# Attention stretches of two head pairs with sixteen products between, in a masked-attention and graph-convolution kernel

## Chip, cores and metric

The kernel runs on one core of a Trainium2 chip. The metric is the device time of one launch in microseconds (us); lower is better.

## What is computed

For each of 32 batches, `x` has 512 rows of 512 features; one 512 x 512 adjacency `adj` serves all. The reference, cut to what matters:

```python
# layer 0: attention with 8 heads of 64, masked by adj
q, k, v = x @ Wq + bq, x @ Wk + bk, x @ Wv + bv
scores = einsum('bihd,bjhd->bhij', q, k) / 8 + where(adj == 0, -1e9, 0)
out = einsum('bhij,bjhd->bihd', softmax(scores), v)
x = layernorm(x + out)
# layer 1: graph convolution with the normalized adjacency
norm_adj = adj * rsqrt(deg)[:, None] * rsqrt(deg)[None, :]
x = layernorm(x + einsum('nm,bmo->bno', norm_adj, x @ weight) + bias)
```

## The kernel before, in words

Everything is in the function `unshifted`. The wrapper `InOrder` pins the instructions of TensorE (PE, matmuls), VectorE (DVE), ScalarE (ACT) and GpSimd (POOL) to the order in which the program issues them; since every one of them passes through its line 44, the profile shows L44 for all, and groups are told apart by their tiles. SyncE (SP) issues nearly all DMAs.

**Blocks.** The work of attention is cut into `S` = 128 blocks: `blocks[k]` is batch `b` = k // 4 and one pair of heads (`ORDER`, line 821); `at` = k % 4. `G` is 4. A block has these parts:

- `scores((b, g, jj))`, lines 395 to 409, is called for jj 0 and 1. Each call makes two score tiles of 128 x 1024 (two heads by 512 columns). PE multiplies with 64 rows of the array for each head (`sc<-kq`), DVE takes the tile out of PSUM with the mask (`e<-sc,maskT`), ACT makes the exponential in place (`e<-e`). PSUM has three "wide" buffers (`WIDE`, bufs=3) for these tiles; SBUF has six `e` buffers.
- `values((b, g, jj))`, lines 430 to 468, multiplies V with the exponentials, with 64 columns of the array for each head (`av<-e,v`). After jj = 1, DVE transposes the result into the single buffer `yb`, and four DMAs carry it to `YT`.
- `accumulate`, lines 411 to 428, sums the exponentials on POOL (`acc`). The sums of the first call are made at once; those of the second are put on the list `pending`, and a piece `put_off` of the side work makes one of them (`more`, line 814). What is left is made at the start of the next block.
- `fold`, lines 470 to 480, transposes and reduces `acc` on DVE (`acc<-acc`, `folded<-acc`), one block later.

**Products.** Between the blocks PE does the projections of the next batch and the graph convolution of the last one. A piece of side work that counts more than 1 is a product: one PSUM bank filled by eight matmul instructions of 128 rows and 128 columns and evicted by DVE or ACT. `bank` (line 98) gives products PSUM buffers in a fixed turn: the three wide ones, then a narrow one. A batch has 32 products: seven for V (`values_of`), seven for each half of K and Q (`keys_and_queries`), four with the adjacency (`first` of `convolve`, eight matmuls of 512 columns each), seven with the second weight (`second`).

**The order.** The loop over k (line 847) is written out by hand. In the turn of block k the program issues `scores` 0 of k, `fold` of k - 1, `scores` 1 of k, `values` 0 and 1 of k - 1, `accumulate` 0 of k, and then `shares.pop(0)`, one share of side work. At `at` = 1 a batch's side work is planned: `main` lists the products, `beside` (a dictionary by the index of the product) says which small steps follow which product, and `cut(side, counts)` (line 799) cuts the list into shares of so many products. Before, each of four blocks gets a share of eight. There too, SP is given the loads of `x` and of the residual.

**The steps in `beside` that matter here** belong to the layer norm of batch b - 1 (`finish`, line 520): `inverse` and `scale` (DVE) divide by the sums, `add` (POOL) adds the residual, `measure` (DVE, `st`, `mv`) takes the statistics, `root` (DVE `ve`, `nmu`, then POOL `rstd`, `add`) makes scale and shift, `norm` (ACT) writes `yT` and the rounded part `hi`, `low` (DVE) writes the rest `lo`. `rest` holds `measure`, `root` and `store` of the convolution before. A `keys_and_queries` product 0 is evicted by ACT into `e1` (`e<-mm,bias`), and product 1 of the same seven adds its bank to that `e1` on DVE (`kq<-e,mm`).

The functions that the change touches, with the line numbers of the profile:

Of the kernel before, what the change touches and what calls it, by code (L numbers as in the profile page):

```python
# [49 lines left out]
def unshifted(  # L50
# [32 lines left out]
    G = H // 2  # L83
# [83 lines left out]
    def load_residual(b):  # L167

        if b < B - 2:
            t = acts.tile([P, NT, D], F32, name="xr", tag="zT", bufs=1)  # L170
            R[b] = [t[:, i, :] for i in range(NT)]
        elif b == B - 2:
            t = [acts.tile([P, 2, D], F32, name="xr2", tag=tag, bufs=n) for tag, n in (("x", 1), ("kq", 5))]
            R[b] = [t[i // 2][:, i % 2, :] for i in range(NT)]
        else:
            R[b] = [wk[:, i].rearrange("p u o -> p (u o)") for i in range(NT)]
        for i in range(NT):
            nc.sync.dma_start(R[b][i], x[b, ts(i, P), :])
# [210 lines left out]
    def turns(b):  # L389

        return [(0, turn, (b, 0))], [(0, turn, (b, 1))] + [(0, combine, (b, k)) for k in range(4)]
# [3 lines left out]
    def scores(s):  # L395

        b, g, jj = s
        E[s] = [work.tile([P, 2, N], F32, name="e", bufs=6) for _ in range(2)]
        for l in range(2):
            j = 2 * jj + l  # L400
            e = E[s][l]
            p = psum.tile([P, 2, N], F32, name="sc", **WIDE)
            for k in range(2):
                r = slice(k * HD, (k + 1) * HD)
                tensor.matmul(p[:, k, :], KQ[b, g][r, 0, ts(j, P)], KQ[b, g][r, 1, :], start=True, stop=True)
            vector.scalar_tensor_tensor(
                e, p, CUT, maskT[:, j, None, :].to_broadcast([P, 2, N]), op0=ALU.min, op1=ALU.subtract
            )
            scalar.activation(e, e, AF.Exp)
# [389 lines left out]
    def cut(pieces, counts):  # L799

        lists = [[]]
        left = list(counts)
        for piece in pieces:
            if piece[0] > 1:
                if not left[0]:
                    left.pop(0)
                    lists.append([])
                left[0] -= 1
            lists[-1].append(piece)
        return lists  # L810
# [3 lines left out]
    def more():  # L814

        if pending:
            accumulate(*pending.pop(0))

    put_off = [(0, more, ())]

    ORDER = (0, 2, 1, 3)
    blocks = [(b, g) for b in range(B) for g in ORDER]
    S = len(blocks)
# [22 lines left out]
    shares, rest, within, inner = [], [], [], []  # L846
    for k in range(S + 1):
        b, at = divmod(k, G)
        if at == 1:
            if 1 < b < B - 1:  # L850
                load_residual(b - 1)
            if b + 2 < B:
                load_x(b + 2, 0)
            if b + 1 < B:
                main, kq = keys_and_queries(b + 1, 0), keys_and_queries(b + 1, 1)
                if b:
                    main = values_of(b + 1) + main
                turn0, turn1 = turns(b + 2) if b + 2 < B else ([], [])
                main += kq[:5]
            if b == 0:  # L860
                w1_parts = [(0, weigh_part, (w1, gpsimd, i)) for i in range(4)]
                exact = [(0, compare, (m,)) for m in range(NT)]
                main += kq[5:]
                beside = {
                    0: exact[:1], 2: put_off, 3: put_off + exact[1:2], 6: put_off + [(0, degrees, ())],
                    7: w1_parts[:1] + put_off, 8: w1_parts[1:2], 9: w1_parts[2:3], 10: put_off + turn0,
                    11: put_off + w1_parts[3:], 12: exact[2:3],
                }
                inner, rest = turn1, exact[3:]
                side = early[5:6] + put_off + early[6:] + put_off  # L870
                side += sum(([piece] + beside.get(i, []) for i, piece in enumerate(main)), [])
                shares = cut(side, (4, 4, 4, 4))
            elif b < B - 1:
                f, c = finish(b - 1), convolve(b - 1)
                norm, low, grow, measure = f["norm"], f["low"], f["grow"], f["measure"]


                beside = {
                    0: rest[:1] + put_off, 1: put_off + rest[1:3], 2: rest[3:4], 3: rest[4:5] + f["inverse"],
                    4: rest[5:6] + f["scale"][:2], 5: rest[6:7] + f["scale"][2:] + f["add"], 6: rest[7:],  # L880
                    8: measure[:2] + put_off, 9: measure[2:] + f["root"] + put_off, 10: norm[:1], 11: norm[1:2],
                    12: norm[2:3] + low[:1], 13: low[1:2], 14: norm[3:] + low[2:3], 16: low[3:] + put_off,
                    17: put_off, 18: f["lift"] + turn0 + f["judge"],
                }
                side = sum(([piece] + beside.get(i, []) for i, piece in enumerate(main)), [])
                side += c["first"] + c["parts"] + grow + kq[5:] + turn1[:1]
                s = c["second"]
                if b < B - 2:
                    side += put_off + s[:1] + put_off + s[1:3] + turn1[1:2] + s[3:4] + turn1[2:3] + s[4:5]
                    side += turn1[3:4] + s[5:6] + c["measure"][:1] + turn1[4:] + s[6:]  # L890
                    rest = c["measure"][1:] + c["root"] + c["store"]
                    shares = cut(side, (8, 8, 8, 8))
                else:
                    held, h, last = c, s, finish(b)
                    scale, add = last["scale"], last["add"]
                    side += h[:1] + last["inverse"] + h[1:2] + scale[:2] + h[2:3] + scale[2:] + add
                    shares = cut(side, (8, 8, 8, 4))
            else:
                f, c, last = last, convolve(b - 1), finish(b)
                s, first, low, lift, pairs = c["second"], c["first"], f["low"], f["lift"], last["pairs"]  # L900
                within = low[:1]
                shares = [
                    h[3:4] + f["measure"] + f["root"] + h[6:] + f["norm"] + f["judge"],
                    h[4:5] + low[1:3] + h[5:6] + low[3:] + lift + put_off + put_off + last["early"] + first[:2]
                    + held["measure"][:2] + first[2:3] + held["measure"][2:] + first[3:] + c["parts"] + f["grow"],
                    held["root"] + s[:2] + pairs[0] + pairs[1],
                    [],
                ]


        while pending:
            more()
        if k == S - 2:
            load_residual(B - 1)
        if k < S:
            scores((*blocks[k], 0))
        else:
            turn_of["n"], turn_of["order"] = 0, (WIDE, dict(tag="narrow"), dict(tag="av"))
        if k == 0:
            run(two)  # L920
            early = values_of(1)
            run(early[:2])
        elif at == 1 and b:
            run(inner)
            inner = []
        if k and blocks[k - 1][0] < B - 1:
            fold(*blocks[k - 1])
        if k < S - 3:
            scores((*blocks[k], 1))
            turn_of["n"] = 0  # L930
        if k:
            values((*blocks[k - 1], 0))
            if k == S:
                sums(B - 1, 1)
            values((*blocks[k - 1], 1))
            if k == S - 2:
                sums(blocks[k - 1][0], (k - 1) % G // 2)
                run(within)
        if k < S and k != S - 2:
            accumulate((*blocks[k], 0))  # L940
        if S - 3 <= k < S:
            scores((*blocks[k], 1))
            turn_of["n"] = 0
        if k == S - 2:
            pending += [((*blocks[k], jj),) for jj in range(2)]
        elif k < S:
            if b == B - 1:
                accumulate((*blocks[k], 1))
            else:
                pending += [((*blocks[k], 1), (l,)) for l in range(2)]  # L950
        if k == S - G - 1:
            load_residual(B - 2)
        if k == 0:
            run(early[2:4] + put_off + put_off + early[4:5])
        elif shares:
            run(shares.pop(0))

    end, e = last, convolve(B - 1)
    norm, low, lift, block, pairs, extend = end["norm"], end["low"], end["lift"], e["block"], end["pairs"], c["extend"]
# [311 lines left out]
```

## Time and profile before

| what | value |
|---|---|
| runs | 2784.51, 2785.0, 2785.21 us; median 2785.0 us |
| profiled execution, time | 2786.06 us |
| its span, first to last instruction | 2784.3 us |
| busy share of the span | PE 99%, DVE 80%, POOL 64%, ACT 38% |
| granted TensorE clock | 0.999 |
| score evictions on DVE | 512 of 1216 ns |
| exponentials on ACT | 512 of 1057 ns |
| sums on POOL | 248 of 2407 ns, 126 of 2368 ns |

The span is what the trace covers; the time of a run is 1.8 us longer in the profiled execution. A busy PE is a PE with matmuls in its pipeline, which includes their filling and draining. One line of the timeline merges equal instructions that follow each other: its start, the length of all of them, the engine, the operation with what it writes and reads, and in brackets the idle time of the engine before it and what ended it. PEld is the loading of weights, which runs beside the matmuls. An f32 matmul appears as two records.

### The profile page before, as it was taken

The numbers are of one execution on the slowest core, as the hardware profiler recorded it, in microseconds if no ns is written. First come the engines' busy times: TensorE is split into PE (matmuls) and PEld (weight loads), VectorE is DVE, ScalarE is ACT, GpSimd is POOL, SyncE is SP. The second block draws the span as 40 slices with busy tenths as digits, with TensorE's granted clock in tenths as the row PEclk, the third lists the DMA queues.
The fourth block names the chain that finished last, engine by engine and source line by source line (L and its number), as shares of the span: only waits on it lengthen the run. The fifth ranks groups of instructions, "written<-read, shape, count | busy, mean of one in ns | idle before, by whom it ended". The sixth has DMA issues, their size and how long they took to land. (4 is left out here: it accounts for less than half of the span.)

```text
span 2784.3 us, 34624 instructions
## 1 busy us (share of the span) xinstructions
PE 2760.3 (99%) x12540; PEld 1877.7 (67%) x12540; DVE 2229.2 (80%) x3204; ACT 1049.8 (38%) x1323; POOL 1794.1 (64%) x1170
## 2 busy tenths in 40 slices
PE   8999999999999999999999999999999999999997
PEld 7666666666666666666666666666666666666655
DVE  5978877788777888777887778877788877788787
ACT  2234333343333433334433334333343433443343
POOL 3666676666666666766667666666666676666756
PEclk9999999999999999999999999999999999999999
DMA  5211222112221211221122211222122122112211
GB/s 121 35 28 48 51 60 57 42 35 53 57 57 43 46 50 50 58 45 42 50 50 61 57 42 35 54 57 57 42 45 50 50 57 46 42 50 50 61 38 51
DMA packets 379109, 141.06 MB, mean 51 GB/s; under 512 B 277808, under 2 KB 345392, under 8 KB 378928
## 3 DMA queue, kind: packets, MB, share of 16 engines
q1 hardware_dynamic: 377776, 137.17, 20.6%
q8 instruction: 101, 1.65, 0.3%
q10 hardware_dynamic: 1152, 1.57, 0.2%
q14 instruction: 80, 0.66, 0.1%
HBM read 71.83 MB, written 33.55 MB: 38 GB/s over the span
## 5 line engine op out<-in xcount | busy, mean ns | idle before, releaser
L44 ACT ACTIVATE e<-e 128x1024 f32<-128x1024 f32 x512 | 540.7, 1057 | 852.4 <-DVE e L44 757.2
L44 POOL TENSOR_TENSOR acc<-acc,e 128x1024 f32<-128x1024 f32 x248 | 596.9, 2407 | 155.4 <-ACT e L44 147.9
L44 DVE SCALAR_TENSOR_TENSOR e<-sc,maskT 128x1024 f32<-128x1024 f32 x512 | 601.4, 1216 | 60.9 <-PE sc L44 60.9
L44 POOL TENSOR_TENSOR acc<-e 128x1024 f32<-128x1024 f32 x126 | 298.3, 2368 | 368.9 <-ACT e L44 368.9
L44 PE MATMUL sc<-kq 64*128 64x512 f32 x2048 | 476.3, 603 | 0.5 <-DVE v L44 0.3
L44 PE MATMUL mm<-xT,wk 128*128 128x256 f32 x1792 | 469.5, 384 | 0.0
L44 PE MATMUL av<-e,v 128*64 128x512 f32 x2048 | 467.9, 599 | 0.0
L44 PE MATMUL mm<-xT,wq 128*128 128x256 f32 x1792 | 460.0, 379 | 0.0
L44 PEld LDWEIGHTS mm<-xT,wk 128*128 128x128 f32 x1792 | 332.3, 190 | 118.0 <-DVE e L44 74.7
L44 PE MATMUL mm<-wv,xT 128*128 128x256 f32 x1792 | 401.3, 381 | 2.1 <-POOL wv L44 1.5
L44 PEld LDWEIGHTS mm<-wv,xT 128*128 128x128 f32 x1792 | 335.2, 190 | 72.6 <-DVE e L44 23.5
L44 PEld LDWEIGHTS mm<-xT,wq 128*128 128x128 f32 x1792 | 340.4, 190 | 46.7 <-ACT wq L44 0.4
L44 PEld LDWEIGHTS av<-e,v 128*64 128x64 f32 x2048 | 135.4, 136 | 316.2 <-issue 275.5
L44 PEld LDWEIGHTS sc<-kq 64*128 64x128 f32 x2048 | 183.7, 186 | 229.1 <-issue 142.4
L44 POOL TENSOR_TENSOR yT<-yT,xr 128x512 f32<-128x512 f32 x124 | 153.9, 1273 | 132.7 <-DVE yT L44 132.7
L44 PE MATMUL mm<-w,zT 128*128 128x256 f32 x992 | 224.7, 379 | 0.0
L44 DVE TENSOR_TENSOR kq<-u,mm 128x512 f32<-128x512 f32 x128 | 87.7, 685 | 161.2 <-PE mm L44 158.1
L44 PEld LDWEIGHTS mm<-w,zT 128*128 128x128 f32 x992 | 188.2, 190 | 27.2 <-DVE wq L44 0.9
L44 PE MATMUL mm<-adjT,hi 128*128 128x512 f32 x496 | 201.8, 407 | 0.0
L44 PE MATMUL mm<-adjT,lo 128*128 128x512 f32 x496 | 196.4, 396 | 0.3 <-DVE lo L44 0.3
L44 DVE TENSOR_TENSOR e<-e,mm 128x512 f32<-128x512 f32 x224 | 151.3, 675 | 48.7 <-PE mm L44 48.6
L44 POOL TENSOR_TENSOR xT<-xT 128x512 f32<-128x512 f32 x126 | 159.3, 1276 | 38.5 <-DVE xT L44 31.8
(145 smaller groups left out, 3212.7 us busy)
## 6 DMA issues: line engine op xcount, KB each, us to landing
out_dram<-y SPq DMA_DIRECT2D x127, 256.0 KB, 2.1
x<-in_x_dram SPq DMA_DIRECT2D x248, 128.0 KB, 2.9
yT<-yb SPq DMA_DIRECT2D x496, 64.0 KB, 2.5
xr<-in_x_dram SPq DMA_DIRECT2D x122, 256.0 KB, 3.4
wk<-in_L_gnn_Wk_dram SPq DMA_DIRECT2D x8, 128.0 KB, 5.0
wq<-in_L_gnn_Wq_dram SPq DMA_DIRECT2D x8, 128.0 KB, 4.3
yT<-in_adj_dram SPq DMA_DIRECT2D x1, 1024.0 KB, 6.0
w<-in_L_gnn_weight_dram SPq DMA_DIRECT2D x2, 512.0 KB, 7.5
```

Of the source, the lines that this page charges most:

```text
L44: return self.tc.keep_in_program_order(op(*args, **kwargs))
```

## The change

For k from 4 to 123, blocks are taken two by two: no products stand between an even block and the odd one after it, and sixteen stand after the odd one. In an odd block both `scores` calls stand ahead of `fold`. The plan's small steps are moved to other products, since the cuts are elsewhere: the put-off sums to products 0, 1, 16 and 17, `measure` and `root` of the layer norm from products 8 and 9 to 9 and 10, the first `norm` from 10 to 11, the steps of `rest`, `inverse`, `scale` and `add` by one; the first three `low` stay at 12, 13 and 14. Batch 0 gives its sixteen products in shares of 4, 4 and 8 where it had four of 4, and the late transposes of its plan (`inner`) run in block 4, not 5.

```diff
-                shares = cut(side, (4, 4, 4, 4))
+                shares = cut(side, (4, 4, 8))
...
                 beside = {
-                    0: rest[:1] + put_off, 1: put_off + rest[1:3], 2: rest[3:4], 3: rest[4:5] + f["inverse"],
-                    4: rest[5:6] + f["scale"][:2], 5: rest[6:7] + f["scale"][2:] + f["add"], 6: rest[7:],
-                    8: measure[:2] + put_off, 9: measure[2:] + f["root"] + put_off, 10: norm[:1], 11: norm[1:2],
-                    12: norm[2:3] + low[:1], 13: low[1:2], 14: norm[3:] + low[2:3], 16: low[3:] + put_off,
-                    17: put_off, 18: f["lift"] + turn0 + f["judge"],
+                    0: rest[:1] + put_off, 1: rest[1:2] + put_off, 2: rest[2:3], 3: rest[3:4],
+                    4: rest[4:5] + f["inverse"], 5: rest[5:6] + f["scale"][:2],
+                    6: rest[6:7] + f["scale"][2:] + f["add"], 7: rest[7:], 9: measure[:2],
+                    10: measure[2:] + f["root"], 11: norm[:1], 12: norm[1:2] + low[:1], 13: norm[2:3] + low[1:2],
+                    14: norm[3:] + low[2:3], 16: low[3:] + put_off, 17: put_off,
+                    18: f["lift"] + turn0 + f["judge"],
                 }
...
-                    shares = cut(side, (8, 8, 8, 8))
+                    shares = cut(side, (16, 16))
...
-                    shares = cut(side, (8, 8, 8, 4))
+                    shares = cut(side, (16, 8, 4))
...
+        double = G <= k < S - G
...
-        elif at == 1 and b:
+        elif k == G:
             run(inner)
-            inner = []
+        if double and at % 2:
+            scores((*blocks[k], 1))
         if k and blocks[k - 1][0] < B - 1:
             fold(*blocks[k - 1])
         if k < S - 3:
-            scores((*blocks[k], 1))
+            if not (double and at % 2):
+                scores((*blocks[k], 1))
             turn_of["n"] = 0
...
-        elif shares:
+        elif shares and (at % 2 or not double):
             run(shares.pop(0))
```

## The prediction

> **What bounds the kernel now.** I read the page first. TensorE (PE) is busy everywhere, VectorE (DVE) four fifths of the time.
>
> ```profile
> PE 2760.3 (99%) x12540; PEld 1877.7 (67%) x12540; DVE 2229.2 (80%) x3204; ACT 1049.8 (38%) x1323; POOL 1794.1 (64%) x1170
> PE   8999999999999999999999999999999999999997
> ```
>
> So time changes only where PE stops, or where it pays for something besides streaming. The chain of waits is no help (it holds only the last 0.8 us). I took the timeline of one stretch of attention (start us, length, engine, what; in brackets the idle time before it):
>
> ```profile
> 1001.45 3.70 PE L44 MATMUL sc<-kq 64*128 64x512 f32 x16
> 1002.62 2.36 DVE L44 SCALAR_TENSOR_TENSOR e<-sc,maskT 128x1024 f32<-128x1024 f32 x2 [1.19 <-PE sc L44]
> 1003.90 0.42 PEld L44 LDWEIGHTS sc<-kq 64*128 64x128 f32 x4 [0.44 <-DVE e L44]
> 1004.90 1.24 DVE L44 STREAM_TRANSPOSE acc<-acc 128x1024 f32<-128x1024 f32 x1
> 1005.08 3.65 PE L44 MATMUL av<-e,v 128*64 128x512 f32 x16
> 1006.17 1.22 DVE L44 TENSOR_REDUCE folded<-acc 128x32 f32<-128x1024 f32 x1
> 1007.30 2.35 DVE L44 SCALAR_TENSOR_TENSOR e<-sc,maskT 128x1024 f32<-128x1024 f32 x2
> 1008.67 1.13 PE L44 MATMUL mm<-xT,wk 128*128 128x256 f32 x4
> 1009.57 0.71 DVE L44 STREAM_TRANSPOSE yb<-av 128x512 f32<-128x512 f32 x1
> ```
>
> PE spends 7.22 us (1001.45 to 1008.67) on four score tiles and the values. DVE starts 1.17 us later and needs until 10.28 - 1.45 = 8.83 us: two evictions, the fold (transpose, reduce), two evictions, the transpose of the values. It is behind, but eight products follow and hide that. The fourth score tile already waits for the first eviction (weight load after 0.44 us idle): a tight bank. Then the end of a run of products that holds a layer norm:
>
> ```profile
> 1015.37 0.16 DVE L44 TENSOR_SCALAR nmu<-mv 128x4 f32<-128x4 f32 x1
> 1016.88 0.81 ACT L44 ACTIVATE yT<-yT,add,rstd 128x512 f32<-128x512 f32 x1 [6.13 <-POOL add L44]
> 1020.64 0.72 ACT L44 ACTIVATE hi<-yT,dis 128x512 fp32r<-128x512 f32 x1
> 1021.27 0.82 ACT L44 ACTIVATE e<-mm,bias 128x256 f32<-128x256 f32 x2
> ...
> 1022.68 3.70 PE L44 MATMUL sc<-kq 64*128 64x512 f32 x16
> 1022.86 0.69 DVE L44 TENSOR_TENSOR kq<-e,mm 128x512 f32<-128x512 f32 x1 [0.71 <-ACT yT L44]
> 1023.85 2.35 DVE L44 SCALAR_TENSOR_TENSOR e<-sc,maskT 128x1024 f32<-128x1024 f32 x2 [0.31 <-PE sc L44]
> ```
>
> Six steps of ScalarE (ACT) follow the statistics; they end 1.5 us before the last eviction (1022.86) becomes possible, so the next stretch's first eviction is on time (1023.85, 1.17 after the scores' start). Last, near the end two stretches already stand back to back:
>
> ```profile
> 2687.48 1.99 PE L44 MATMUL sc<-kq 64*128 64x512 f32 x8
> 2689.40 3.65 PE L44 MATMUL av<-e,v 128*64 128x512 f32 x16
> 2692.98 1.99 PE L44 MATMUL sc<-kq 64*128 64x512 f32 x8
> 2694.90 3.72 PE L44 MATMUL mm<-w,parts 128*128 128x256 f32 x16
> ```
>
> **What the Trainium skill says.** "TensorEngine Tiling (Array Packing)", Key Properties: "Mode switching requires drain". The trace agrees: a product record starts every 0.216 us, but the first scores start 0.31 after the last product, and their first step takes 0.53, not 0.43. The same page, PSUM Bottleneck, says that tiling does not speed up the evacuation of PSUM: here a score tile takes PE 0.86 us and DVE 1.22. "TensorE: Matmul & The Clock Gate", Architectural detail: ScalarE and VectorE are strict first in, first out; in the trace the third score tile is complete at about 1004.3, and its eviction starts at 1007.30 behind the fold, as the program orders it (it needs an `e` buffer too, so this is no proof).
>
> **The change part by part.** S is the score start of the first block of a double stretch; the order of the changed program's instructions gives what follows what.
>
> *Mode changes.* Before, a stretch costs on entering 0.31 - 0.216 = 0.09 and 0.53 - 0.43 = 0.10, on leaving 0.10 (values to product) and 0.10 (first product 0.32, not 0.216): 0.40. A double drops one such pair and adds values to scores: 3.58 us from 2689.40 to 2692.98, as from values to products (1005.08 to 1008.67), so 0.10, and 0.10 for the first step (1.92 for four steps of 0.43). Saved: 0.20 per double. k runs from 4 to 123, 60 doubles: -11.8 us.
>
> *The eighth score tile.* Three wide banks: tile 8 of a double takes tile 5's. Tile 5 is written from S + 7.22 on; DVE is free at S + 8.74 (its next instruction can start some 0.09 before the transpose of the values ends at 8.82), so tile 5's eviction ends at 8.74 + 1.21 = 9.95. Before, the fourth tile's weight load came 0.05 after the first eviction; at 2.46 us from its scores' start it cost nothing, at 2.58 it cost 0.01, at 3.07 (one early stretch) 0.50: PE loses what exceeds 2.57. Here it comes at 10.00 - 7.22 = 2.78: PE loses 0.21, and the values and all products queue behind it. Where the stretch follows the second half of a batch (last evictions of `y`), DVE is late by 0.13 in the trace of before too (first eviction at +1.31 in place of +1.18): 0.34 there.
>
> *Evictions 7 and 8.* They need an `e` buffer (six, eight tiles), so the values of the block and the POOL sum of it. They come at about S + 12.2 and 13.3, before the products need these banks (first product at 14.7 takes a free bank, the second is 1.8 later): nothing on PE; behind them on DVE wait the fold and the values' transpose. DVE then ends the stretch at 17.6, 0.9 later against its products than before; four product banks of 1.73 us each cover it, and before DVE idled over 1 us in such a run. SP: the loads of x and residual at at == 1 now stand between the two blocks' `yb` DMAs; `yb` has one buffer, its four DMAs are issued in 2.65 us from S + 8.85 and land 2.5 us after, about 14, ahead of the second use at 16.9: nothing. The POOL sums of the first block run from 4.8 to 13, before their fold; those put off behind the products are the same two. The `y` stores (ACT 0.80 each, then a DMA on SP) move one product later, to about product 8, and the buffer that they free is wanted at product 12, 7 us on: nothing.
>
> *The layer norm in the first long run.* This I think decides. All sixteen products of a batch's first run are now continuous, and `measure` stands one product later (behind products 9 and 10, not 8 and 9), while `low` stays at 12. Take R for the time when product 15 can be evicted (0.18 after the next scores' start; before 1022.86). Product 10 can be evicted at R - 5 x 1.728 = R - 8.64. Product 9's eviction (R - 10.37) and two statistics of 0.82 put product 10's (two `u`, 0.78) at R - 8.13; two more statistics and `ve` put `nmu` at R - 5.52. Before it was at 1015.37 - 1022.86 = R - 7.49. From `nmu` to the third `hi` it takes 1021.36 - 1015.37 = 5.99: now R + 0.47. Behind it ACT evicts product 14 (`e<-mm,bias`, 0.82, beginning 0.09 early): R + 1.20. Product 15's `kq` reads that `e` and starts at R + 1.25, and the first score eviction 0.60 later, R + 1.85, not R + 0.99 (1023.85): late by 0.86. The queued scores then wait: the fourth tile's weight load comes at 1.18 + 0.86 + 1.22 + 0.05 = 3.31 after the scores' start; PE loses 3.31 - 2.57 = 0.74. The rest of that double is 0.86 late on DVE and 0.74 on PE, so tile 8 costs 0.21 + 0.12 = 0.33.
>
> *Sum of a batch.* First double 0.34 + 0.01 (its fourth tile), second 0.74 + 0.33: 1.42 lost, 2 x 0.197 saved: +1.02. Batches 1 to 30: +30.7 us. Batch 0 runs 4, 4, 8 products in place of 4, 4, 4, 4, and the late transposes (`inner`) move from k = 5 to 4: below 1 us by their rows (1.24 us once), set to nothing, bound -1 to +2.
>
> The profiled execution took 2786.06 us, its span 2784.3 and 1.8 around it; plus 30.7 that is 2816.8, and since the median shown is 1.1 lower (2785.0), I take **2815**.
>
> Bounds: the tile-8 wait is not in the trace of before. It is nothing if DVE's evictions follow each other 0.35 us sooner, and at most 0.3 more if PE also has to refill after it: -16 to +18 us over 60. The norm chain could hide wholly (0.86 us of slack found): 0 to -26; or POOL's residual adds, which end about 1 us before the last statistics need them, come later by 1 us too: +30.
>
> **The rivals.** *Only mode changes count* (faster): no bank waits, since DVE catches up before tile 8. Place: tile 5's eviction; it decides if that ends before S + 9.74. Price -0.197 x 60: 2773. For it: the 0.21 is small beside a double of 42 us. Against: DVE's five steps and the values' transpose are back to back in the trace. *Bank wait alone*: the norm chain is hidden, 0.35 + 0.21 - 0.39 = +0.17 per batch: 2790. For it: 0.7 us idle before 1022.86. Against: that is less than the 1.97 by which the chain moves. *DVE never catches up in the first run*: its 0.9 us backlog adds to the norm's lateness and to POOL's adds, 30 x 0.9: 2842. Against: product 3 finds DVE idle by my count. That the order isn't what the title says is excluded: PE's order has scores, values, scores, values, then sixteen products.
>
> **Numbers.** My case (2800 to 2828) 0.60; bank wait alone 0.13; DVE backlog 0.15; mode changes alone 0.12. I set the range to 2787 to 2838. A change of 0.2% (5.6 us) is about what can be told from none: faster 0.11, same 0.06, slower 0.83.
>
> **What would show it.** Right: PE idle "<- DVE e" at the fourth score tile of every second double (0.7) and at the eighth of every double (0.2 to 0.35); `kq` waiting for ACT before it; from values to scores 0.52 us from last to first start; PE busy time unchanged. Wrong: no weight-load wait beyond 0.1 us in the stretches, or the waits inside the products.

## The result, and the profile after

The changed kernel takes 2810.83 us (median of four runs, 2810.58 to 2811.19) where the kernel before takes 2785.07 us: ratio 1.0093, 95% interval 1.008 to 1.0106. It is slower by 25.8 us, against a forecast of 30. The profiled execution's span grew from 2784.3 to 2809.2 us. The page shows almost nothing of it; PE's share is the same, and its busy time grew by 13 us with the same matmuls:

```profile
PE 2773.4 (99%) x12540; PEld 1875.7 (67%) x12540; DVE 2239.2 (80%) x3204; ACT 1049.9 (37%) x1323; POOL 1784.7 (64%) x1170
PE   9999999999999999999999999999999999999997
```

The table of waits (who waited for whom: us in total, times, longest) says where to look. First the changed kernel, then the kernel before:

```profile
PEld sc L44 <- DVE e L44: 172.6, 248, 1.6
PE sc L44 <- DVE e L44: 10.7, 32, 0.7
```

```profile
PEld sc L44 <- DVE e L44: 61.6, 128, 1.1
```

The weights of score tiles wait for evictions 248 times, not 128. The total is not the price: most of these waits are idle time of the weight load, which runs ahead of the matmuls and may be late for a while at no cost. The price is read from the starts of the matmuls. Here are lines, chosen from the timeline, of the end of a first long run in the changed kernel and of the double stretch behind it (start, length, engine, what, idle time before it):

```profile
1019.01 0.16 DVE L44 TENSOR_SCALAR nmu<-mv 128x4 f32<-128x4 f32 x1
1020.51 0.81 ACT L44 ACTIVATE yT<-yT,add,rstd 128x512 f32<-128x512 f32 x1 [8.19 <-POOL add L44]
1024.28 0.72 ACT L44 ACTIVATE hi<-yT,dis 128x512 fp32r<-128x512 f32 x1
1024.48 2.85 PE L44 MATMUL sc<-kq 64*128 64x512 f32 x12
1024.90 0.82 ACT L44 ACTIVATE e<-mm,bias 128x256 f32<-128x256 f32 x2
1025.03 0.75 DVE L44 SCALAR_TENSOR_TENSOR lo<-yT,dis,hi 128x512 fp32r<-128x512 f32 x1 [0.70 <-ACT hi L44]
1025.76 0.69 DVE L44 TENSOR_TENSOR kq<-e,mm 128x512 f32<-128x512 f32 x1
1026.36 2.35 DVE L44 SCALAR_TENSOR_TENSOR e<-sc,maskT 128x1024 f32<-128x1024 f32 x2
1027.63 0.30 PEld L44 LDWEIGHTS sc<-kq 64*128 64x128 f32 x4 [1.14 <-DVE e L44]
1027.64 1.13 PE L44 MATMUL sc<-kq 64*128 64x512 f32 x4 [0.31 <-DVE e L44]
1028.69 3.65 PE L44 MATMUL av<-e,v 128*64 128x512 f32 x16
1032.28 4.02 PE L44 MATMUL sc<-kq 64*128 64x512 f32 x16
1033.30 0.71 DVE L44 STREAM_TRANSPOSE yb<-av 128x512 f32<-128x512 f32 x1
1033.93 2.32 DVE L44 SCALAR_TENSOR_TENSOR e<-sc,maskT 128x1024 f32<-128x1024 f32 x2
1035.16 0.30 PEld L44 LDWEIGHTS sc<-kq 64*128 64x128 f32 x4 [0.87 <-DVE e L44]
1036.23 3.65 PE L44 MATMUL av<-e,v 128*64 128x512 f32 x16
1037.42 2.35 DVE L44 SCALAR_TENSOR_TENSOR e<-sc,maskT 128x1024 f32<-128x1024 f32 x2 [1.18 <-PE av L44]
1039.81 1.13 PE L44 MATMUL mm<-xT,wk 128*128 128x256 f32 x4
```

Both waits are there. The third `hi` ends at 1025.00, after the scores began at 1024.48. From there two ways lead to `kq`: ACT's eviction of product 14, which `kq` reads, runs to 1025.72, and DVE, which had waited 0.70 us for that `hi`, writes `lo` up to 1025.78. `kq` stands behind both and starts at 1025.76, so the first score eviction starts 1.88 us after the scores, not 1.18. The scores' sixteen records split into 12 and 4: the fourth tile starts at 1027.64, 0.48 late, and its second step another 0.10 late. From scores to values it is 4.21 us (1024.48 to 1028.69) in place of 3.63: **0.58 us lost at the fourth tile**. In the second block it is 1036.23 - 1032.28 = 3.95, so **0.31 us lost at the eighth tile**, whose weights waited until 1035.16 for tile 5's eviction (begun at 1033.93). PE's idle column shows 0.31 of the first loss and none of the second: the modelled end of the matmul before covers the rest, which is why its busy time grew. DVE's wait of 1.18 at 1037.42 for an `e` buffer cost PE nothing: the products began at 1039.81, 3.58 after the values.

Over the trace, scores to values takes 4.22 or 3.64 in the first blocks of doubles by turns, and 3.95 in the second blocks, but for two early blocks (4.98 and 4.95). Summed over what exceeds 3.63, 19.1 us lie in the first blocks and the single stretches and 19.8 in the second blocks, 38.9 in all; the kernel before had 1.6. The mode changes gave back 60 x 0.197 = 11.8. 38.9 - 1.6 - 11.8 = 25.5, against 24.9 in the span: nothing else of size is in it.

### The profile page after: what moved, and what is told of

Same layout as the page of the kernel before. It is cut to its first block, busy times and chain, and to the rows that moved or that the text cites. A ratio compares the mean times of both kernels' runs of the same rounds, so it can differ in the third digit from the quotient of the medians.

```text
span 2809.2 us, 34651 instructions
## 1 busy us (share of the span) xinstructions
PE 2773.4 (99%) x12540; PEld 1875.7 (67%) x12540; DVE 2239.2 (80%) x3204; ACT 1049.9 (37%) x1323; POOL 1784.7 (64%) x1170
## 5 line engine op out<-in xcount | busy, mean ns | idle before, releaser
L44 POOL TENSOR_TENSOR acc<-acc,e 128x1024 f32<-128x1024 f32 x248 | 586.8, 2366 | 92.2 <-ACT e L44 77.7
L44 PE MATMUL sc<-kq 64*128 64x512 f32 x2048 | 500.8, 612 | 13.3 <-DVE e L44 10.7
L44 PE MATMUL mm<-xT,wk 128*128 128x256 f32 x1792 | 463.3, 381 | 0.0
L44 PEld LDWEIGHTS sc<-kq 64*128 64x128 f32 x2048 | 176.1, 186 | 302.7 <-DVE e L44 172.6
L44 ACT ACTIVATE y<-y,add,rstd 128x512 f32<-128x512 f32 x127 | 96.1, 806 | 285.9 <-POOL add L44 285.9
L44 DVE SCALAR_TENSOR_TENSOR lo<-yT,dis,hi 128x512 fp32r<-128x512 f32 x124 | 152.5, 1231 | 59.2 <-ACT hi L44 55.9
```

Source lines behind the costliest of these rows:

```text
L44: return self.tc.keep_in_program_order(op(*args, **kwargs))
```

## The experiments

The theory: three terms. Mode changes saved (-11.8), the bank wait at the eighth tile, and the late layer norm before every second double. The rivals: VectorE's backlog in the long run, a cost of PE itself in having scores behind values, and mode changes that save nothing (a mode is the split of PE's array: whole, 64 rows or 64 columns for each head). All ratios are to the kernel before, 2784.9 us in these runs.

**e1: the small steps, those of the layer norm among them, where they stood before.** Double stretches as in the changed kernel.

```diff
 beside = {
-    0: rest[:1] + put_off, 1: rest[1:2] + put_off, 2: rest[2:3], 3: rest[3:4],
-    4: rest[4:5] + f["inverse"], 5: rest[5:6] + f["scale"][:2],
-    6: rest[6:7] + f["scale"][2:] + f["add"], 7: rest[7:], 9: measure[:2],
-    10: measure[2:] + f["root"], 11: norm[:1], 12: norm[1:2] + low[:1], 13: norm[2:3] + low[1:2],
-    14: norm[3:] + low[2:3], 16: low[3:] + put_off, 17: put_off,
+    0: rest[:1] + put_off, 1: put_off + rest[1:3], 2: rest[3:4], 3: rest[4:5] + f["inverse"],
+    4: rest[5:6] + f["scale"][:2], 5: rest[6:7] + f["scale"][2:] + f["add"], 6: rest[7:],
+    8: measure[:2] + put_off, 9: measure[2:] + f["root"] + put_off, 10: norm[:1], 11: norm[1:2],
+    12: norm[2:3] + low[:1], 13: low[1:2], 14: norm[3:] + low[2:3], 16: low[3:] + put_off, 17: put_off,
...
```

> Double stretches as in the changed kernel, but the small steps stand at the products where they stood before (statistics behind products 8 and 9). If the late layer norm costs 0.58 us in every second double (30 x 0.58 = 17.5), it falls to about 2793 us and the wait at the fourth score tile of those doubles goes; the wait at the eighth tile (0.31) stays. If the norm's place does not matter and the first long run is simply too full for VectorE (rival: backlog), it stays at 2811 with the same wait at the fourth tile.

Measured: 2787.92 us, ratio 1.001 (1.0002 to 1.0019), 22.9 us less than the changed kernel. The timeline of e1 behind a first long run:

```profile
1015.70 3.70 PE L44 MATMUL sc<-kq 64*128 64x512 f32 x16
1015.88 0.69 DVE L44 TENSOR_TENSOR kq<-e,mm 128x512 f32<-128x512 f32 x1 [0.71 <-ACT yT L44]
1016.88 2.35 DVE L44 SCALAR_TENSOR_TENSOR e<-sc,maskT 128x1024 f32<-128x1024 f32 x2 [0.31 <-PE sc L44]
1019.33 3.65 PE L44 MATMUL av<-e,v 128*64 128x512 f32 x16
1022.92 3.90 PE L44 MATMUL sc<-kq 64*128 64x512 f32 x16
1025.68 0.30 PEld L44 LDWEIGHTS sc<-kq 64*128 64x128 f32 x4 [0.75 <-DVE e L44]
1026.74 0.65 PE L44 MATMUL av<-e,v 128*64 128x512 f32 x2
```

The last product is evicted 0.18 us after the scores start, as in the kernel before, the first score eviction is on time (1.18), and the fourth tile loses nothing (1015.70 to 1019.33 is 3.63). The run of sixteen products is as full as it was, so the backlog rival falls. It gained 5 us more than expected. Most of that is the eighth tile's loss, which did not stay: in these doubles it fell from 0.31 to 0.19 (1022.92 to 1026.74 is 3.82). Over the trace the losses at the fourth tiles fell by 18.4 us and those at the eighth by 3.8, together 22.2 of the 22.9.

**e2: the fold moved behind the first half of the second block.**

```diff
         if double and at % 2:
+            fold(*blocks[k - 2])
             scores((*blocks[k], 1))
-        if k and blocks[k - 1][0] < B - 1:
+        if k and blocks[k - 1][0] < B - 1 and not (double and at % 2 == 0):
             fold(*blocks[k - 1])
```

> Changed kernel, with the fold of the block before a double moved from the even block to the odd one, between its two calls of scores. VectorE can then take tiles 3 and 4 about 1 us sooner and reaches tile 5 before its bank is wanted. If the eighth tile waits for that bank, 60 x 0.31 = 19 us go: about 2792 us, with 0.58 left at the fourth tile of every second double. Rival (the loss at the eighth tile is a cost of PE itself, of scores after values): 2811 as before, with the gap at the eighth tile unchanged.

Measured: 2791.73 us, ratio 1.0024 (1.0015 to 1.0034), 19.1 less than the changed kernel, as the bank theory said. A second block of e2:

```profile
1025.04 3.70 PE L44 MATMUL sc<-kq 64*128 64x512 f32 x16
1026.21 2.35 DVE L44 SCALAR_TENSOR_TENSOR e<-sc,maskT 128x1024 f32<-128x1024 f32 x2 [0.34 <-PE sc L44]
1027.49 0.42 PEld L44 LDWEIGHTS sc<-kq 64*128 64x128 f32 x4 [0.44 <-DVE e L44]
1028.67 1.51 PE L44 MATMUL av<-e,v 128*64 128x512 f32 x6
```

DVE takes tile 5 as soon as PE has it (1026.21), the weights of the eighth tile come 2.45 us after the scores' start, and scores to values is 3.63 us here and in all second blocks. PE still goes from values straight to scores, so it was no cost of PE in that order.

**e3: both.**

> Both: steps of the layer norm at their old products, and the fold in the odd block. My account leaves only the saved mode changes, 60 x 0.197 = 11.8 us below the kernel before: about 2773 to 2775 us, faster than before. Rival (mode changes are worth nothing, a drain is paid in any case): 2785.

Measured: 2772.6 us, ratio 0.9955 (0.9942 to 0.9969): faster than both kernels, 12.3 us below the kernel before. A double stretch of e3:

```profile
1017.39 3.70 PE L44 MATMUL sc<-kq 64*128 64x512 f32 x16
1021.03 3.65 PE L44 MATMUL av<-e,v 128*64 128x512 f32 x16
1024.61 1.13 PE L44 MATMUL mm<-xT,wk 128*128 128x256 f32 x4
```

```profile
1014.93 2.35 DVE L44 SCALAR_TENSOR_TENSOR e<-sc,maskT 128x1024 f32<-128x1024 f32 x2 [1.23 <-PE av L44]
1017.51 0.72 DVE L44 STREAM_TRANSPOSE yb<-av 128x512 f32<-128x512 f32 x1 [0.22 <-PE av L44]
1018.57 2.35 DVE L44 SCALAR_TENSOR_TENSOR e<-sc,maskT 128x1024 f32<-128x1024 f32 x2 [0.34 <-PE sc L44]
1020.84 1.23 DVE L44 STREAM_TRANSPOSE acc<-acc 128x1024 f32<-128x1024 f32 x1
1022.11 1.22 DVE L44 TENSOR_REDUCE folded<-acc 128x32 f32<-128x1024 f32 x1
1023.25 2.34 DVE L44 SCALAR_TENSOR_TENSOR e<-sc,maskT 128x1024 f32<-128x1024 f32 x2
```

DVE now waits for PE (0.34 at 1018.57) and not PE for DVE; the second block takes 3.64 and 3.58 us like a single stretch. The fold fills the time in which evictions 7 and 8 have to wait for an `e` buffer anyway. The sum fits: 11.8 from mode changes and 0.7 from waits at score tiles (0.9 us above 3.63 are left in e3, 1.6 before) make 12.5, against 12.3 between the medians. (The spans of the profiled executions differ by 13.4; that of the kernel before was 1.1 us slower than its median.) In its waits, "PEld sc <- DVE e" still stands with 110.3 us, 188 times, and costs next to nothing: the 0.9 us are all that was lost at score tiles.

**e4: the kernel before, with the small steps moved as in the changed kernel.** Single stretches; the put-off sums stay behind products 8 and 9.

```diff
-    0: rest[:1] + put_off, 1: put_off + rest[1:3], 2: rest[3:4], 3: rest[4:5] + f["inverse"],
-    4: rest[5:6] + f["scale"][:2], 5: rest[6:7] + f["scale"][2:] + f["add"], 6: rest[7:],
-    8: measure[:2] + put_off, 9: measure[2:] + f["root"] + put_off, 10: norm[:1], 11: norm[1:2],
-    12: norm[2:3] + low[:1], 13: low[1:2], 14: norm[3:] + low[2:3], 16: low[3:] + put_off, 17: put_off,
+    0: rest[:1] + put_off, 1: rest[1:2] + put_off, 2: rest[2:3], 3: rest[3:4],
+    4: rest[4:5] + f["inverse"], 5: rest[5:6] + f["scale"][:2],
+    6: rest[6:7] + f["scale"][2:] + f["add"], 7: rest[7:], 8: put_off, 9: measure[:2] + put_off,
+    10: measure[2:] + f["root"], 11: norm[:1], 12: norm[1:2] + low[:1], 13: norm[2:3] + low[1:2],
+    14: norm[3:] + low[2:3], 16: low[3:] + put_off, 17: put_off,
...
```

> The kernel before, single stretches, with nothing changed but the places of the small steps: statistics behind products 9 and 10 as in the changed kernel. If the norm's place alone makes the next first score eviction late by 0.7 us, it costs 30 x 0.58 = 17 us without any double stretch: about 2802 us. Rival (it needs the full first run of sixteen products): 2785.

Measured: 2803.86 us, ratio 1.0068 (1.0054 to 1.0082), 18.9 us above the kernel before. The stretch behind such a run in e4:

```profile
507.66 0.81 ACT L44 ACTIVATE yT<-yT,add,rstd 128x512 f32<-128x512 f32 x1 [7.98 <-POOL add L44]
511.43 0.72 ACT L44 ACTIVATE hi<-yT,dis 128x512 fp32r<-128x512 f32 x1
511.62 2.85 PE L44 MATMUL sc<-kq 64*128 64x512 f32 x12
512.18 0.75 DVE L44 SCALAR_TENSOR_TENSOR lo<-yT,dis,hi 128x512 fp32r<-128x512 f32 x1 [0.71 <-ACT hi L44]
512.91 0.69 DVE L44 TENSOR_TENSOR kq<-e,mm 128x512 f32<-128x512 f32 x1
513.51 2.35 DVE L44 SCALAR_TENSOR_TENSOR e<-sc,maskT 128x1024 f32<-128x1024 f32 x2
514.78 1.13 PE L44 MATMUL sc<-kq 64*128 64x512 f32 x4 [0.32 <-DVE e L44]
515.84 2.37 PE L44 MATMUL av<-e,v 128*64 128x512 f32 x10
```

It is the same picture without any double stretch: first eviction at 1.89, scores to values 4.22. One early stretch lost 1.3 us more than in the kernel before, and 30 x 0.58 = 17.4 is the rest. So it is the places of the small steps. The edit moves several of them; that `measure` and `root` decide is read from the trace: ACT's first `yT` waits 7.98 us for the shift `add` that follows `nmu`, so it is not the place of `norm` that holds it. No run moves these two alone.

**e5: the changed kernel with the fold first in the odd block.** This undoes one part of the change.

```diff
-        if double and at % 2:
-            scores((*blocks[k], 1))
         if k and blocks[k - 1][0] < B - 1:
             fold(*blocks[k - 1])
         if k < S - 3:
-            if not (double and at % 2):
-                scores((*blocks[k], 1))
+            scores((*blocks[k], 1))
```

> Changed kernel with one part undone: in an odd block the fold stands ahead of the second call of scores again, as in every other block. The fold needs the POOL sums of the even block, which I put at 13.1 us after the even block's scores; so evictions 7 and 8 end near 16.8 and 18.0 us in place of 13.4 and 14.6, while products 1 and 2 want their banks at 16.6 and 18.3. My account expects some 0.3 us of PE waiting at product 1 of each double, 60 x 0.3 = 18: about 2829 us. Rival (the product banks cover the later evictions): 2811. A second rival (without VectorE's wait for the values ahead of eviction 7 it gains): below 2808.

Measured: 2844.22 us, ratio 1.0212 (1.0198 to 1.0226), 33 us above the changed kernel. The place was right, the size too small:

```profile
1052.34 1.25 DVE L44 STREAM_TRANSPOSE acc<-acc 128x1024 f32<-128x1024 f32 x1 [2.08 <-POOL acc L44]
1053.62 1.22 DVE L44 TENSOR_REDUCE folded<-acc 128x32 f32<-128x1024 f32 x1
1054.75 2.35 DVE L44 SCALAR_TENSOR_TENSOR e<-sc,maskT 128x1024 f32<-128x1024 f32 x2
```

```profile
1054.79 1.03 PE L44 MATMUL mm<-xT,wq 128*128 128x256 f32 x4
1056.02 1.13 PE L44 MATMUL mm<-xT,wk 128*128 128x256 f32 x4 [0.21 <-DVE e L44]
```

The fold waits 2.08 us for POOL's sums, eviction 7 ends later for it, and the second product, whose bank it holds, starts at 1056.02 in place of 1055.65, 0.37 late, with 0.10 more at its next record. (An f32 product is four matmul instructions and so eight records, 0.216 apart; the second half of the first product starts at 1054.79.) That is 0.47 us in every second double. In the others it is 0.53, but for the first double of all, which lost 5.2: over the trace 34 us, against 33 measured. So the calls of `scores` side by side in the odd block are a part of the change that it needs.

## Why the prediction was right

The direction, the places and the mechanism held: VectorE is late at two score tiles, and PE loses that time. The sum was too large by 5 us. (2785.0 and 30.7 make 2815.7; the forecast of 2815 is that without its fraction.)

- *Mode changes*: the changed kernel has 62 changes from values to scores where before there were 2, each 0.52 us from last to first start and 0.53 for the first step, as worked out. e3, in which little else is left, is 12.3 us faster against 11.8.
- *The eighth tile*: forecast 0.34 and 0.33, measured 0.31 and 0.31; e1, where DVE is on time behind the first long run, shows 0.19 for the bare wait that was put at 0.21. e2 shows that it is VectorE's lateness at the bank and not PE's order.
- *Evictions 7 and 8*: DVE waits 1.18 us for the `e` buffer, and PE loses nothing. e5 shows where that ends: 3.3 us later (8.46 us after the second block's scores in place of 5.14) it costs about 0.5 a double.
- *The layer norm*: the mis-sized term. R is again the time when product 15 can be evicted, 0.18 after the scores' start. `nmu` was put at R - 5.52 and came at R - 5.65 (1019.01, R = 1024.66), `kq` at R + 1.10, not R + 1.25. The first eviction was late by 0.71, not 0.86, so PE lost 0.58 at the fourth tile, not 0.74. These 0.16 us a batch make 4.8 us of the 4.9 between 30.7 and 25.8. That they fit so closely is luck in part: the eighth tiles were put too high as well, by 0.05 us a batch (1.5 us), and once-only losses early in the program, which the prediction set at nothing, made up for about 1 us (block 5, behind the moved `inner`, lost 1.32 us at its eighth tile in place of 0.31). Of the lateness 0.13 arose ahead of `nmu`: product 9's eviction, the statistics and the two `u` followed each other that much sooner than I had added up from their rows.
- *The backlog*: DVE was to be idle by product 3, and nearly was: it evicts that product at 1003.64, and ahead of the next one it stands idle for 1.23 us (it waits for POOL's `u`). So no backlog reaches the layer norm, and e1 excludes the rival.

```profile
1003.64 0.69 DVE L44 TENSOR_TENSOR u<-e,mm 128x512 f32<-128x512 f32 x1
1005.71 0.69 DVE L44 TENSOR_TENSOR v<-u,mm 128x512 f32<-128x512 f32 x1 [1.23 <-POOL u L44]
```

- *What was to show it*: the matmul starts have the losses at the fourth and eighth tiles as forecast, and 0.52 us from values to scores. Three signs did not come as put. PE's idle column has 0.31 at the fourth tile and nothing at the eighth. PE's busy time rose (2773.4, not 2760.3), as the modelled ends cover part of the waits, so this sign was badly chosen. And `kq` does not wait for ACT: DVE waits one instruction earlier, ahead of `lo`. The prediction followed only the way through ACT's eviction of product 14. Both ways start from the third `hi` and end within 0.06 us of each other (1025.72 and 1025.78), so the sum came out the same; that is luck. By these ends, taking one of the two away would have gained almost nothing; no run tried it.

"Mode switching requires drain" (the Trainium skill, "TensorEngine Tiling (Array Packing)", Key Properties) agrees with all traces here: they show what a change costs, not what PE does in it. From the last start of one kind to the first of the next there are 0.09 us more than inside a kind, and the first step behind the change is longer, by 0.10 us for scores and products and by 0.05 for values (0.48, not 0.43). So a change costs 0.20 us into scores or products and 0.14 from scores to values. A double saves one of 0.20. The evacuation of PSUM, which the same page (PSUM Bottleneck) says tiling does not speed up, takes back 0.31.

## What to carry to other kernels

Before two stretches of a bound engine are joined, write out what the second engine did behind the gap between them: here eight products had hidden the tail of VectorE's eight microseconds, and only with the fold moved into another wait, and the layer norm's steps put back, did the joining gain (e3). Recheck each small step whose place is counted in products: a shift by one product of 1.73 us decided whether the layer norm's chain was over before the scores (e4). And price a wait from the start times of the bound engine; a table of waits shows idle time that costs nothing beside idle time that does.

## What the runs showed of the hardware

The weight load of the last score tile of a block (the fourth or the eighth) could be up to 0.12 us later than usual (2.57 in place of 2.45 us from the scores' start) at no cost. When it was later, PE lost the lateness beyond that: 0.19 us at 2.76 (e1), 0.31 at 2.88 and 0.58 at 3.15 (the changed kernel). Of each loss 0.10 us came only with the following step, which takes 0.53 and not 0.43 us.
